# A six-block perceiver kernel: second ternary product from two float32r parts, norm weights applied while transposes are emptied, three scan states weighted outside VectorE

## The chip, the core and the metric

The kernel runs on one core of a Trainium2 chip. The metric is the device time of one launch in microseconds (us), the median of several runs. A core has five instruction queues that run side by side and wait for each other by semaphores: TensorE (PE, with its weight loads listed apart as PEld), VectorE (DVE), ScalarE (ACT), GpSimd (POOL) and SyncE (SP), which here issues all transfers. Each queue runs its instructions strictly in the order in which the program holds them.

## What is computed

128 sequences of 32 latent rows with 256 features (`x`) pass six residual blocks; each sequence also has a context of 257 rows with 256 features. Cut to what matters here:

```python
x = x + softmax_attention(ctx, layernorm(x))            # L0_xattn: latents attend to the context
x = x + mamba(layernorm(x))                             # L0_attn: per channel, 16 states
#   h = h * exp(A * d_t) + (x_t * d_t) * B ;  y_t = h @ C[0] ;  gate * (y + x*D) @ W_out + b
x = x + ternary_mlp(layernorm(x))                       # L0_ffn
#   h = gelu(x @ Wq_fc.T) ; h = layernorm(h)*ln_w + ln_b ; h @ Wq_proj.T   (Wq in {-1,0,1})
x = x + linear_attention(layernorm(x), ctx, ctx)        # L1_xattn
#   k = relu(ctx @ Wk + bk) + eps, scaled; k <- k^3 / |k^3| * |k| ; v = ctx @ Wv + bv
#   kv = k^T v ; z = 1 / (q . sum(k) + eps) ; out = (q kv) * z
x = x + latent_attention(layernorm(x))                  # L1_attn, 16 heads, decay on the scores
x = x + quantized_mlp(layernorm(x))                     # L1_ffn: 8-bit activations, ternary weights
```

All of it is float32 on the outside; the two linear maps of `quantized_mlp` run on whole numbers in bfloat16.

## The kernel before

The 4096 latent rows are 32 groups of 128 rows (four sequences to a group). Groups are taken in blocks of `BLOCKS = (2, 4, 4, 4, 4, 4, 4, 4, 2)`. A block goes through three stages: `context_group` for each of its groups (softmax attention over the context, then the keys and values of the later linear attention, `keys` and `keys_values`, which leave one small matrix `kvc` per group), `scan_block` for the block as a whole (four chunks `ic` of 128 channels, 16 states each), and `latent_group` for each group (`mlp`, `linear`, `attention`, `quantized_mlp`).

The order of instructions isn't the order of the text. Every call goes to a `Recorder`; `order` is a planner that places the recorded operations one by one. It has a price list for instructions (`ns_of`), due times for each part of the work (the table `DUE`), and factors (`PRICE`, `WINDOW` and others) with which it picks the next operation and, where an operation may run on several engines (`either`, `scaled`, `relu`, `copy`, `cast`, `minus_column`), its engine. Its result is a fixed order for each queue. Where the planner sees TensorE idle for longer than `GAP`, `keep_busy` puts in filler matmuls of constants (`onesb`, `identb`). All recorded instructions are issued from one line of the helper, so the profile shows L587 for them all, and they are told apart by the names of their tiles.

What the steps below touch:

- `cubed` (from L777): the scale `f` of a cubed key row from two sums of squares, `kn` (`ln` for queries): one GpSimd power of both sums (`kn<-kn,halves`), then their product (`kf<-kn`). `keys_values` (L1134) makes `u` (tile `ku`): ScalarE relu of the product `pkey`, GpSimd add of `e1`, two ScalarE squares with a row sum, GpSimd product, two squares again; then `vf`, the values scaled by `f`, and matmuls into `pk`.
- `context_group` (L1005) makes `kvc` from `pk` with two VectorE instructions.
- `norm` (L981): subtracts the row mean and multiplies by `rstd` on VectorE (`xn`). Used by `scan_block`, `attention` and `quantized_mlp`.
- `scan_block` (L1172): for each state `s`, ScalarE makes the decay `a`, VectorE runs the scan `h`. For `s < POOLED` GpSimd multiplies `h` by its weight and adds it to `some`; for the others VectorE does both in one instruction into `acc`. `POOLED` is 2, and `LATE_POOLED`, 6, in the last two blocks.
- `mlp` (L1240): the first ternary product (`ph<-w_fc,xT`) already takes its rows as two float32r parts. Then GELU (`hid`), eight transposes, two ScalarE copies out of PSUM (`hT`), eight float32 matmuls with `w_pr` (`pmlp`), into which `late_setup` has multiplied `ln_w` and from which it has taken the column mean.
- `linear` (L1276): `den`, `zf` and `y`, with the value bias `bv1` multiplied by the denominator on GpSimd.
- `quantize` and `quantized_mlp` (L1426, L1458): `xn` is multiplied by the factor `qm` and rounded; `q` is the bfloat16 result.

A float32 matmul shows as two records in the profile, a float32r or bfloat16 matmul as one. `R.together()` makes matmuls one unit for the planner.

Of the kernel before, what the change touches and what calls it, by code (L numbers as in the profile page):

```python
# [17 lines left out]
P = 128  # L18
# [24 lines left out]
def ns_of(engine, name, kw, out, ins, n):  # L43

    if engine == "vector":
# [4 lines left out]
        if name == "bn_aggr":  # L50
            return 118
        if name == "reciprocal":
            return 65 + 6.6 * n
        if name in ("tensor_scalar", "tensor_copy", "scalar_tensor_tensor"):
# [3 lines left out]
            start = (105 if in_psum(ins[0]) else 65) if both else 92  # L58
            return start + (0, 60, 175)[pointers] + (0.52 if fast else 1.04) * n
        return max(75 + 1.04 * n, 150)  # L60
    if engine == "scalar":
        pointers = is_ap(kw.get("scale")) + is_ap(kw.get("bias"))
        if n == BB * (LQ - 1):
            return 655
        rate, start = (0.834, 85) if in_psum(ins[0]) else (0.93, 65)
        return start + 75 * pointers + rate * n + (135 if kw.get("accum_out") is not None else 0)
    if engine == "gpsimd":
        if kw.get("op") == ALU.pow:
            return 400 + 150 * n
        if name in ("memset", "tensor_copy"):  # L70
            return 190 + 0.7 * n
        if name == "tensor_scalar":
            pointers = sum(is_ap(kw.get(k)) for k in ("scalar1", "scalar2"))
            return 195 + 75 * pointers + 0.83 * n
        if n == NH * LQ and shown(ins[1]).ap[-1][0] == 0:
            return 1030
        return 200 + (2.07 if n < 1000 else 1.7) * n
    if engine == "tensor":
# [7 lines left out]
        if not wide:  # L86
            return max(n / 2.4 + 3, 60)
# [180 lines left out]
class Recorder:  # L268
# [79 lines left out]
    def cost(self, engine, name, args, kw, all_reads, all_writes, all_bufs):  # L348
        if True:
            out = kw.get("out", args[0] if args else None)  # L350
            rest = list(args[1:] if "out" not in kw else args)
            rest += [v for k, v in kw.items() if k not in ("out", "accum_out")]
            ins = [a for a in rest if is_ap(a)]
            outs = [a for a in (out, kw.get("accum_out")) if is_ap(a)]
            full = dict(kw)
            if name == "tensor_scalar":
                full |= dict(zip(("scalar1", "scalar2"), args[2:4]))
            if name == "scalar_tensor_tensor":
                full |= dict(zip(("scalar",), args[2:3]))
            if name == "activation":  # L360
                full |= dict(zip(("func",), args[2:3]))
            if engine == "gpsimd" and name == "tensor_tensor":
                full |= dict(zip(("op",), args[3:4]))
            n = size_of(out)
            ns = ns_of(engine, name, full, out, ins, n)
            table = TABLES.get(full.get("func")) if name == "activation" else None
            tensors = [
                a for a in ins if (size_of(a) > 1 or name == "tensor_tensor") and not in_psum(a)
            ]
            locks = engine == "gpsimd" and len(ins) > 0  # L370
            if engine == "vector":
                two = name in ("tensor_tensor", "scalar_tensor_tensor", "tensor_tensor_scan")
                fast = name in ("tensor_scalar", "tensor_copy") and not in_psum(out)
                locks = len(tensors) > 1 if two else fast and len(tensors) > 0 and n > 64
# [228 lines left out]
PRICE = {"tensor": 0.0, "vector": 45.207809, "scalar": 8.002797, "gpsimd": 6.895979, "sync": 0.0}  # L603
WINDOW = 13.504066
SOONER = 0.067879
AHEAD = 0.971922
HORIZON = 1.829143
# [3 lines left out]
def perceiver_kernel(ctx: ExitStack, tc: tile.TileContext, t: dict, out: bass.AP):  # L611
# [30 lines left out]
    nc.gpsimd.memset(halves[:, 1, :], 0.5)  # L642
    ones = cst.tile([P, P], F32, name="ones")
# [58 lines left out]
    def t4k(shape, name):  # L702
        return ring("t4", 4).tile(shape, name)

    def t2k(shape, name, dtype=F32):
        return ring("t2", 15).tile(shape, name, dtype)
# [33 lines left out]
    bv1 = row("bv1", t["bv1"], D)  # L740
# [18 lines left out]
    w_pr = wts.tile([P, 8, D], F32, name="w_pr")  # L759
# [911 lines left out]
```

## Time and profile before

| | |
|---|---|
| time, median of 3 runs | 1727.35 us (1726.26 to 1727.77) |
| the profiled execution: its own time | 1720.31 us |
| its span, first to last instruction | 1718.6 us |
| DVE scans `h<-a,pproj` | 576 instructions, 615.9 us |
| ACT decays `a<-dl,a_neg` | 576, 368.9 us |
| PE `pval` and `pkey` records | 2 x 1024, 243.5 and 238.1 us |
| PE `pmlp` records | 512, 116.8 us |
| ACT table loads | 91, 116.8 us |
| DMA | 59.72 MB, mean 35 GB/s |

A group's busy time is the union of its instructions' spans; "mean" is one instruction's span from start to end. Instructions that follow each other on a queue overlap a little, so the time that one takes from its queue is a little less than its span. PE spans hold the latency to the result: a 256-column matmul of bfloat16 has a span of 0.27 us and starts 0.11 us after the one before it. So PE can show as busy while it waits. The 1.71 us between the span and the execution's own time lie outside the first and the last instruction.

### The profile page before, as it was taken

Reading aid. Unit: us, or ns where it says so; the run is one execution under the profiler, and the core shown is the slowest. Engines: PE = TensorE matmul, PEld = TensorE weight load, DVE = VectorE, ACT = ScalarE, POOL = GpSimd, SP = SyncE. Lnnn points to the kernel's source line nnn. Section 1 sums busy time; section 2 is a strip of 40 time slices with the busy share of each in tenths; the row PEclk is TensorE's granted clock in tenths of the full one; section 3 lists DMA queues with packets and bytes.
Section 4 is the critical chain, followed back from the end, with each engine's and each line's share of the span. In section 5 each row is a group of like instructions: output and inputs, shape, how many; then the busy total and the mean of one; then the engine's idle time right before and its main releaser. Section 6 shows DMA issues by size and latency. Waiting matters only on the chain.

```text
span 1718.6 us, 45554 instructions
## 1 busy us (share of the span) xinstructions
PE 1636.2 (95%) x17465; PEld 1209.2 (70%) x17495; DVE 1513.6 (88%) x2992; ACT 1406.5 (82%) x3441; POOL 1311.0 (76%) x2063
## 2 busy tenths in 40 slices
PE   9999999999999999999999999999999988888897
PEld 6777667767777777777777777766777656666664
DVE  5499599989997799969999998989999899999787
ACT  4588698979887898979988889888987888777676
POOL 6668667867688678887788777867887789688787
PEclk9999999999999999999999999999999999999999
DMA  8221100110110101000210011001100000000000
GB/s 252 79 76 60 30 28 30 35 58 1 35 57 2 35 14 57 8 30 13 70 29 30 4 45 55 10 30 35 42 35 30 2 11 16 4 5 2 5 9 22
DMA packets 44761, 59.72 MB, mean 35 GB/s; under 512 B 8704, under 2 KB 27008, under 8 KB 44544
## 3 DMA queue, kind: packets, MB, share of 16 engines
q1 hardware_dynamic: 44544, 56.81, 10.4%
q8 instruction: 138, 2.26, 0.6%
q14 instruction: 79, 0.65, 0.1%
HBM read 52.32 MB, written 4.19 MB: 33 GB/s over the span
## 4 chain that ended last, share of the span: by engine, by line
PE 41%; DVE 25%; ACT 16%; POOL 13%; issue 5%; DVEq 0%; POOLq 0%; ACTq 0%
DVE h L587 10%; PE pkey L587 7%; DVE acc L587 7%; PE pval L587 6%; PE pproj L587 5%; POOL ku L587 3%; ACT a L587 3%; PE pT L587 3%; PE pmlp L587 2%; ACT L587 2%; POOL some L587 2%; PE pk L587 2%; ACT ks L587 2%; PE pqa L587 2%; POOL rstd L587 1%
## 5 line engine op out<-in xcount | busy, mean ns | idle before, releaser
L587 DVE TENSOR_TENSOR_SCAN h<-a,pproj 128x512 f32<-128x512 f32 (+1 forms) x576 | 615.9, 1087 | 21.6 <-ACT a L587 11.2
L587 ACT ACTIVATE a<-dl,a_neg 128x496 f32<-128x496 f32 (+1 forms) x576 | 368.9, 665 | 82.7 <-DVE h L587 79.3
L587 DVE SCALAR_TENSOR_TENSOR acc<-h,w_st,acc 128x512 f32<-128x512 f32 (+1 forms) x436 | 299.2, 686 | 0.9
L587 PE MATMUL pval<-wkv,cT 128*128 128x256 f32 x1024 | 243.5, 383 | 2.8 <-DVE x L587 1.8
L587 PE MATMUL pkey<-wkv,cT 128*128 128x256 f32 x1024 | 238.1, 386 | 0.0
L587 ACT ACTIVATE ks<-ku 128x256 f32<-128x256 f32 x512 | 209.2, 414 | 13.6 <-POOL ku L587 10.2
L587 PEld LDWEIGHTS pkey<-wkv,cT 128*128 128x128 f32 x1024 | 189.3, 190 | 37.9 <-issue 14.8
L587 PEld LDWEIGHTS pval<-wkv,cT 128*128 128x128 f32 x1024 | 188.3, 190 | 35.3 <-issue 4.5
L587 POOL TENSOR_TENSOR ku<-ku,e 128x512 f32<-128x512 f32 x128 | 164.9, 1298 | 42.9 <-ACT ku L587 41.6
L587 POOL TENSOR_TENSOR ku<-ks,ku 128x512 f32<-128x512 f32 x128 | 163.2, 1283 | 20.5 <-ACT ks L587 18.9
L587 POOL TENSOR_TENSOR kn<-kn,halves 128x4 f32<-128x4 f32 x128 | 131.2, 1027 | 17.9 <-ACT ks L587 16.7
L587 ACT ACTIVATE vf<-pval,kf 128x256 f32<-128x256 f32 x256 | 107.8, 474 | 30.8 <-PE pval L587 17.5
L587 POOL TENSOR_TENSOR rstd<-rstd,halves 128x1 f32<-128x1 f32 x224 | 124.3, 558 | 7.0
L587 PE MATMUL pproj<-xTs,w_in 128*128 128x512 f32 (+1 forms) x288 | 123.7, 554 | 1.3 <-ACT vf L587 0.7
L587 ACT ACT_TABLE_LOAD x91 | 116.8, 1283 | 2.0 <-PE ph L587 0.5
L587 PE MATMUL pmlp<-w_pr,hT 128*128 128x256 f32 x512 | 116.8, 381 | 1.5 <-ACT hT L587 1.2
L587 POOL TENSOR_TENSOR some<-some,h 128x512 f32<-128x512 f32 (+1 forms) x104 | 115.1, 1107 | 3.1
L587 POOL TENSOR_SCALAR h<-h,w_st 128x512 f32<-128x512 f32 (+1 forms) x104 | 65.0, 628 | 60.4 <-DVE h L587 50.1
L587 POOL TENSOR_SCALAR rstd<-mv 128x1 f32<-128x1 f32 x224 | 45.5, 203 | 84.7 <-DVE mv L587 56.1
L587 PEld LDWEIGHTS pmlp<-w_pr,hT 128*128 128x128 f32 x512 | 95.8, 190 | 17.0 <-ACT hT L587 2.1
L587 ACT ACTIVATION_READ_ACCUMULATOR ks<-ku 128x1 f32 x512 | 100.1, 195 | 0.0
L587 ACT ACTIVATE ku<-pkey 128x512 f32<-128x512 f32 x128 | 73.0, 592 | 14.8 <-PE pkey L587 11.7
(289 smaller groups left out, 3836.1 us busy)
## 6 DMA issues: line engine op xcount, KB each, us to landing
cx<-in_ctx_dram SPq DMA_DIRECT2D x64, 512.0 KB
x<-in_x_dram SPq DMA_DIRECT2D x32, 128.0 KB
cr<-in_ctx_dram SPq DMA_DIRECT2D x128, 32.0 KB
out_dram<-x SPq DMA_DIRECT2D x32, 128.0 KB
vlz<-vl SPq DMA_DIRECT2D x128, 1.1 KB
w_in<-in_w_inT_dram SPq DMA_DIRECT2D x1, 1024.0 KB
raw_fc<-in_w_fcT_dram SPq DMA_DIRECT2D x2, 512.0 KB
raw_pr<-in_w_prT_dram SPq DMA_DIRECT2D x2, 512.0 KB
```

What stands on the lines that cost most here:

```text
L587: ins = getattr(engine, name)(*(traced(a) for a in args), **{k: traced(v) for k, v in kw.items()}).ins
```

## The change

- `mlp`: each half of the transposed `hid` leaves PSUM in four instructions of 128 columns, each multiplied by its part of `ln_w` (now rows on partitions); a copy to float32r (`hi`) and the difference (`lo`) follow; `pmlp` is 16 float32r matmuls with the ternary `w_pr`. The mean of the normalized rows is taken off behind the product, by one more VectorE instruction with `s1`. In `ph` the matmuls run part by part.
- `norm` is gone. The row mean is taken out of the weights (`centred` for `w_in`, `w_gate`, `wqa`, `wkd`) and rows are only scaled (`normed`), on VectorE, GpSimd or ScalarE as the planner picks. `scan_block` computes `rstd` for its groups in one pair of GpSimd instructions (`rs4`). `quantized_mlp` only subtracts the mean, and `rstd` goes into `amax` and `qm`.
- `POOLED` is 3, and the multiplication of a pooled state may run on ScalarE.
- `cubed`: VectorE reciprocal of one sum, a product, one power. In one of four sequences (`WHOLE`) VectorE does relu and add in one instruction. `kvc` gets the value bias at once (`bvc`, `vb`), and `linear` drops `den` and two of its steps. `bvc` comes by 16 transfers of 16 x 16 elements instead of one.
- The planner's price list, factors and due times are new, so the order changes everywhere. The ring `t4` has 3 buffers (4 before), `t2` has 17 (15 before).

The diff, cut to its core:

```diff
@@ cubed
-        powers = halves[:, 0:2, 0:n] if inverse else halves[:, 1:3, 0:n]
-        R.gpsimd.tensor_tensor(nrm, nrm, powers, ALU.pow)
         f = tiny(f"{tag}f", [P, n])
-        R.gpsimd.tensor_tensor(f, nrm[:, 0, :], nrm[:, 1, :], ALU.mult)
+        R.vector.reciprocal(f, nrm[:, 1 - inverse, :])
+        R.either.tensor_tensor(f, f, nrm[:, inverse, :], ALU.mult)
+        R.gpsimd.tensor_tensor(f, f, halves[:, 1, 0:n], ALU.pow)
@@ setup
+    centred(w_in, 2)
+    centred(w_gate, 2)
+    centred(wqa, 2)
@@ late_setup
-        R.vector.tensor_tensor(w_pr, w_pr, lnw.unsqueeze(2).to_broadcast([P, 8, D]), ALU.mult)
-        centred(w_pr, 8)
+        for col, dst, sign in ((lnb, s0, 1.0), (lnw, s1, -1.0)):
...
+            R.vector.tensor_scalar(dst, pS[:, 0:D], sign, None, ALU.mult)
@@ norm -> normed
-        xn = t1k([P, D], "xn")
-        R.vector.tensor_scalar(xn, xg, mv[:, 0:1], r, ALU.subtract, ALU.mult)
+    def normed(xg, r):
+        xn = t1k([P, D], "xn")
+        R.record({
+            "vector": ("tensor_scalar", (xn, xg, r, None, ALU.mult), {}),
+            "gpsimd": ("tensor_scalar", (xn, xg, r, 1.0, ALU.mult, ALU.mult), {}),
+            "scalar": ("activation", (xn, xg, AF.Copy), {"scale": r}),
+        })
@@ context_group
-        R.vector.tensor_scalar(kvc, v[:, 0], odd[:, 0:1], None, ALU.mult)
+        R.scaled(kvc, v[:, 0], odd[:, 0:1])
         R.vector.scalar_tensor_tensor(kvc, v[:, 1], odd[:, 1:2], kvc, ALU.mult, ALU.add)
+        vb = t1k([P, 2, GB, 16], "vb")
+        R.either.tensor_tensor(
+            vb, bvc.unsqueeze(2).to_broadcast([P, 2, GB, 16]),
+            kvc[:, :, :, 16:17].to_broadcast([P, 2, GB, 16]), ALU.mult,
+        )
+        R.either.tensor_tensor(kvc[:, :, :, 0:16], kvc[:, :, :, 0:16], vb, ALU.add)
@@ keys_values
+        if whole:
+            R.vector.scalar_tensor_tensor(u, z, 0.0, e12, ALU.max, ALU.add)
+        else:
+            R.relu(u, z)
+            R.gpsimd.tensor_tensor(u, u, e12, ALU.add)
@@ scan_block
                 if s < pooled:
-                    R.gpsimd.tensor_scalar(h, h, weight, 0.0, ALU.mult, ALU.add)
+                    R.record({
+                        "gpsimd": ("tensor_scalar", (h, h, weight, 0.0, ALU.mult, ALU.add), {}),
+                        "scalar": ("activation", (h, h, AF.Copy), {"scale": weight}),
+                    })
@@ mlp
-        hT = t4k([P, 8, P], "hT")
-        transposed(hid, hT, 8)
+        halved = []
+        for k in range(0, 8, 4):
...
+            for j in range(4):
+                R.scaled(hT[:, j, :], pt[:, j * P : (j + 1) * P], lnw[:, k + j : k + j + 1])
+            R.record({
+                "vector": ("tensor_copy", (hi, hT), {}),
+                "scalar": ("copy", (hi, hT), {}),
+                "gpsimd": ("tensor_copy", (hi, hT), {}),
+            })
+            R.either.tensor_tensor(lo, hT, hi, ALU.subtract)
+            halved += [(hi, k), (lo, k)]
         po = bank("pmlp")
         with R.together():
-            accumulate(po[:, 0:D], [(hT[:, c, :], w_pr[:, c, :]) for c in range(8)])
+            accumulate(
+                po[:, 0:D],
+                [(part[:, j, :], w_pr[:, k + j, :]) for part, k in halved for j in range(4)],
+            )
+        R.vector.scalar_tensor_tensor(po[:, 0:D], s1, mv[:, 0:1], po[:, 0:D], ALU.mult, ALU.add)
         R.vector.scalar_tensor_tensor(xg, po[:, 0:D], r2, xg, ALU.mult, ALU.add)
@@ linear
-        R.vector.tensor_copy(den, pv[:, :, 16])
...
-        R.gpsimd.tensor_tensor(
-            yv, bv1.rearrange("p (h k) -> p h k", k=16),
-            den.unsqueeze(2).to_broadcast([P, NH, 16]), ALU.mult,
-        )
-        R.vector.tensor_tensor(yv, pv[:, :, 0:16], yv, ALU.add)
-        R.vector.tensor_tensor(yv, yv, zf.unsqueeze(2).to_broadcast([P, NH, 16]), ALU.mult)
+        R.vector.tensor_tensor(
+            yv, pv[:, :, 0:16], zf.unsqueeze(2).to_broadcast([P, NH, 16]), ALU.mult
+        )
@@ quantize / quantized_mlp
-        R.vector.tensor_scalar(m, m, 127.0, None, ALU.mult)
+        R.either.tensor_scalar(m, m, 127.0, unit, ALU.mult, ALU.mult)
...
+        R.minus_column(xn, xg, mv[:, 0:1])
...
+        R.either.tensor_tensor(amax, amax, r, ALU.mult)
@@ constants
-POOLED = 2
+WHOLE = (0,)
+POOLED = 3
```

## The prediction

> **What bounds the kernel now.** First the page: busy shares, then the chain of work that ended last.
>
> ```profile
> PE 1636.2 (95%) x17465; PEld 1209.2 (70%) x17495; DVE 1513.6 (88%) x2992; ACT 1406.5 (82%) x3441; POOL 1311.0 (76%) x2063
> PE 41%; DVE 25%; ACT 16%; POOL 13%; issue 5%; DVEq 0%; POOLq 0%; ACTq 0%
> ```
>
> No engine sets the end alone: all four are on the chain. Next, busy time by stage, cut where the first scan starts (96 us) and where the last block's scans end (about 1600 us), and one stretch inside.
>
> ```profile
> 0.00:96.00 96.00, 91.57 (x816) 67.80 (x816) 46.44 (x124) 50.47 (x163) 60.44 (x110) 1.00 0.52 161
> 96.00:1600.00 1504.00, 1445.10 (x15241) 1071.28 (x15258) 1373.60 (x2604) 1278.28 (x3123) 1155.79 (x1785) 1.00 0.09 28
> 1600.00:1719.00 119.00, 99.53 (x1417) 70.14 (x1421) 93.55 (x265) 77.79 (x157) 94.73 (x169) 0.99 0.04 13
> 780.00:1180.00 400.00, 392.37 (x4269) 291.69 (x4277) 376.45 (x713) 354.43 (x846) 305.10 (x482) 1.00 0.10 31
> ```
>
> Columns: PE, PEld, DVE, ACT, POOL. In the middle PE shows 96.1% busy, DVE 91.3%, ACT 85.0%, POOL 76.8%; from 780 to 1180 us DVE holds 94.1% and ACT 88.6%. PE and DVE limit the middle together. ACT's longest wait is for DVE, by the view of waits (total, times, longest):
>
> ```profile
> ACT a L587 <- DVE h L587: 79.3, 102, 2.4
> ```
>
> In the tail no engine is full; dependences set the pace, and POOL is at 80%.
>
> **The change, part by part.** Counts are those of the changed program's queues; durations are means of the groups before. From these I take the overlap with the next instruction: 0.1 us on ACT (three decays of 0.50 us in a row take 1.29), 0.08 on DVE (two scans of 0.67 take 1.26).
>
> *PE.* The timeline gives the rates:
>
> ```profile
> 1628.68 3.62 PE L587 MATMUL pmlp<-w_pr,hT 128*128 128x256 f32 x16
> 1620.53 2.08 PE L587 MATMUL ph<-w_fc,xT 128*128 128x512 f32 x8
> 1703.75 1.03 PE L574 MATMUL poq<-onesb,identb 128*128 128x512 bf16 x4
> 1705.42 1.05 PE L587 MATMUL poq<-w,qT 128*128 128x256 bf16 x8 [0.64 <-ACT qT L587]
> ```
>
> Less the last one's span (0.38, 0.39, 0.39, 0.27), starts are 0.216 us apart for a float32 record of 256 columns, 0.241 for float32r of 512 (`ph`), 0.213 for bfloat16 of 512 and 0.111 of 256. The trace has no float32r matmul of 256 columns. Its bounds are 0.111 (bfloat16) and 0.216 (nothing gained per record); I take 0.111 plus the 0.028 that `ph` shows over bfloat16, 0.139. So 512 records of 0.216 become 512 of 0.139: -39 us (bounds -54 and 0). The setup adds six 512-column and two 256-column float32 matmuls (0.87 and 0.43), while eight for `lnw` replace eight for the mean of `w_pr`: +6. 31 fillers fewer (204 to 173) are -7 of busy time that stood in waits. PE's busy time: -40.
>
> [...]
>
> *DVE.* `acc`: 24 of 512 (0.66) and 4 of 256 fewer, -17. `xn` leaves: 96 x 0.415 and 32 x 0.49, -56. `y`, two steps and one back, -14. One `kvc`, `den` and part of `qm`: -14. Added: 161 reciprocals at 0.074, +12; 32 relu-and-adds from PSUM (as `pproj`, 0.67), +21; 32 times `s1` (as `x<-pmlp`, 0.39), +12; setup, five means and five subtractions for four weights, less what `w_pr` needed, +3. Sum -53.
>
> The `xn` means hold stalls: median and longest are in the second figure column.
>
> ```profile
> L587 DVE TENSOR_SCALAR xn<-x,mv,rstd x96: 360/406/1349, 44.4 to 1697.7; 128x256 f32<-128x256 f32 x96
> L587 DVE TENSOR_SCALAR xn<-xn,qm x32: 298/346/4076, 321.3 to 1699.3; 128x256 f32<-128x256 f32 x32
> ```
>
> Against the medians the stalls are 96 x 0.09 + 32 x 0.23 = 16 us of the 56; if they only move to other instructions the sum is -37. [...] The scans show none (longest 1.22 us at a mean of 1.21).
>
> *ACT.* `h` times its weight, 64 of 512 (as `a`, 0.61) and 30 of 256 (0.40): +51. `hT`, 256 of 128 columns: `vf` takes 0.474 at 256, and 128 columns are worth 0.108 by the two sizes of `a`, so 0.266 each: +68, less 64 copies of 0.495, +36 (without the overlap +62). `hi`, 38 of 512 (as `ea`, 0.53): +20. `xn`, 55 at 0.41: +23. `kvc`, 32 at 0.27: +9. 32 fewer relus: -16. Ten table loads fewer: -13. Sum +110, some 4 of it in the tail.
>
> *POOL.* `lo`, 64 x 1.28: +82. `some`, 24 x 1.275 + 4 x 0.73: +34. `hi`, 26 at about 0.6: +16. Smaller additions (mean subtraction, rounding, `vb`, `kvc`, `qm`, `amax`, `rs4`): +95. Removed: 66 weight products, -40; 32 adds of `e1`, -42; `kn` with four powers 1.03, with two 0.72, -39; queries -6; `rstd` -24; `y` -20. Sum +56. In the middle POOL would stand near 81%: hidden.
>
> *New waits.* The scale of a key row now visits DVE (`kf`), behind scans of 1.21 us, and GpSimd's power, ScalarE's `vf` and PE's `pk` queue up behind it. Keys run a stage ahead, and PE waited only 1.8 us for `kf` so far; I take 0. Uncovered, half a scan each is 128 x 0.6 = 77 us. `pmlp` waits for `lo`, and the context matmuls behind it on PE wait too; in the middle that is a matter of order, in the tail it counts below.
>
> *SP.* 15 transfers more at about 0.47 us each are 7 us of queue. Ahead of the first `plg` stand 58 issues, not 51, so it goes out at 39 us, not 36; its matmul started at 60 us. Cost 0; without that cover, 7.
>
> *Sum by stage.* Head: PE's first `w_in` projection has some 3 us less real work before it, but the next seven are spread among later context work: 0 (bounds -7 and +7). Middle, each engine at the density it keeps: PE (1445 - 40) / 0.961 = 1462; DVE (1374 - 53) / 0.913 = 1447; ACT (1278 + 106) / density. ACT becomes the fullest, and its density decides. Its longest wait is for a DVE that has less to do, and DVE shows that 94.1% can be held for 400 us; at that, 1471, or -33. At DVE's mean of 91.3% it is 1516, +12. I take 0.941. Tail: per group +0.5 (`hT`), +0.6 (`hi`), +1.3 (`lo`), +0.4 (`s1`), -1.2 (`pmlp`), -1.0 (`linear`); with POOL carrying 3.6 us more for each of some three groups, +4 (bounds -2 and +11). Together 0 - 33 + 4 = -29 against the profiled execution's 1720.3: 1691. The median of the runs is 7 us above that execution, so 1698.
>
> **The rivals.**
>
> *ACT hides its 110 us* (1690 or less). For it: 15% of the middle is idle on ACT. Against: it would need over 95%. PE then sets the middle, -42, with the tail 1689; with the 0.111 rate, 1674; with a head shorter by 7 too, 1667.
>
> *ACT becomes the bound: slower.* Place: scan stretches, where decays, squares, `vf` and now `h`, `hi` and `hT` share one queue. ACT has not held more than 88.6% in the 400 us shown. It decides from a density in the middle under 1384/1500 = 92.3%. At DVE's 91.3%: +12 + 4, 1743; at 88.6%, 1562, so +62, 1789. Against it: ACT's idle time was largely waiting for the engine that is relieved.
>
> *The float32r product gains nothing* (0.216 each). PE stays at 1445 - 1: 1503 for the middle, with the tail 1730, no change.
>
> **How the numbers follow.** Likeliest case 0.60, own range 1684 to 1722; ACT hides 0.10; ACT bounds 0.20; no gain on PE 0.10. Telling apart from no change takes about 0.2%, so 1723.9 to 1730.8 is "same". Faster: 0.57 + 0.10 + 0.03 = 0.70. Same: 0.02 + 0.02 + 0.04 = 0.08. Slower: 0.01 + 0.18 + 0.03 = 0.22. The range goes from 1662, just under the lowest of the second case, to 1743, the nearer price of the slower one; about 0.15 is left out.
>
> **What would show it.** Right: `pmlp` with 512 records about 0.14 us apart; DVE near 1460 us busy, ACT near 1515, POOL near 1365; ACT's waits for `h` well under 79 us; ACT at 93% or more between 300 and 1300 us. Wrong: `pmlp` starts 0.2 us apart; DVE waiting for `a` for tens of us (11.2 so far); ACT full and PE's waits longer; PE waiting at `pk` for `kf` or at `pmlp` for `lo`; a stretch after 1600 us much over 119 us.

## The result and the profile after

| | before | after |
|---|---|---|
| median of the runs (lowest to highest) | 1726.98 us (1721.69 to 1727.77, 9 runs) | 1731.58 us (1730.49 to 1733.57, 9 runs) |
| ratio to before, 95% interval | | 1.0035 (1.0027 to 1.0044) |
| profiled execution, its span | 1720.31, 1718.6 us | 1732.48, 1730.8 us |
| mean granted TensorE clock in it | 0.999 | 0.984 |

The change made the kernel 0.35% slower; 1698 us had been forecast. The profiled execution of before lies 7 us under its median and that of after 1 us over its own, so the two traces differ by 12 us where the medians differ by 5.

The page of the changed kernel, busy time by engine and then the chain of work that ended last:

```profile
PE 1614.0 (93%) x17484; PEld 1184.9 (68%) x17484; DVE 1467.7 (85%) x2933; ACT 1492.2 (86%) x3810; POOL 1356.1 (78%) x2214
ACT 32%; PE 27%; DVE 21%; POOL 15%; issue 5%; DMA 1%; DVEq 0%; POOLq 0%; ACTq 0%
```

Against before, DVE is down by 46 us (forecast 53), ACT up by 86 (110), POOL up by 45 (56), PE down by 22 (40). The loads moved as forecast, in sign and nearly in size; ACT's share of the chain doubled from 16 to 32%, and the time did not fall. PE and DVE are now busy for a smaller share of the span than before, ACT and POOL for a larger one.

The stretches, cut where the first scan starts, where the last scan starts, and at the end. The columns are PE, PEld, DVE, ACT and POOL busy, then clock, DMA share and GB/s. First the kernel before:

```profile
0.00:96.50 96.50, 92.07 (x848) 68.15 (x849) 46.93 (x124) 50.69 (x163) 60.44 (x110) 1.00 0.52 162
96.50:1609.30 1512.80, 1453.01 (x15393) 1076.66 (x15408) 1382.24 (x2628) 1286.12 (x3142) 1164.04 (x1796) 1.00 0.09 28
1609.30:1718.60 109.30, 91.11 (x1234) 64.42 (x1239) 84.42 (x242) 69.72 (x137) 86.47 (x158) 0.98 0.04 14
```

and the changed kernel, with two inner stretches:

```profile
0.00:83.80 83.80, 79.78 (x709) 59.93 (x710) 46.07 (x124) 42.52 (x142) 51.57 (x98) 1.00 0.49 151
83.80:1614.30 1530.50, 1444.01 (x15618) 1063.94 (x15620) 1348.77 (x2605) 1376.23 (x3517) 1208.94 (x1934) 0.99 0.09 30
1614.30:1730.80 116.50, 90.26 (x1169) 61.01 (x1158) 72.85 (x206) 73.41 (x152) 95.64 (x184) 0.92 0.04 12
300.00:1300.00 1000.00, 964.38 (x10742) 714.50 (x10735) 885.97 (x1679) 912.01 (x2322) 813.58 (x1325) 0.99 0.10 31
1300.00:1500.00 200.00, 170.64 (x1513) 116.08 (x1512) 174.52 (x298) 169.90 (x384) 152.17 (x234) 0.96 0.04 13
```

The head is 12.7 us shorter, the scan stretch 17.7 longer, the tail 7.2 longer: together the 12.2 us between the spans. In the scan stretch ACT was busy for 1376 us, close to the 1384 of the prediction, but in 1530.5 us: 89.9% dense, not 94.1. By the starts of the scans, the blocks keep the pace that they had: from the second block's first scan to the seventh's it is 942 us before and 945 after. What is lost on balance is lost behind 1340 us, and from there on no engine is near full: from 1300 to 1500 us they stand at 76 to 87%.

The view of waits of the changed kernel (total, times, longest):

```profile
POOL vb L588 <- DVE kvc L588: 39.1, 14, 5.3
DVE pproj L588 <- ACT some L588: 34.2, 14, 12.1
ACT a L588 <- DVE h L588: 33.2, 44, 4.8
PEld L575 <- issue: 33.1, 46, 6.2
POOL some L588 <- ACT h L588: 29.6, 19, 5.8
DVE h L588 <- ACT a L588: 24.9, 30, 2.3
```

and two rows of it in the kernel before:

```profile
DVE pproj L587 <- ACT some L587: 20.0, 11, 6.1
DVE h L587 <- ACT a L587: 11.2, 14, 2.1
```

ACT's waits for `h` fell from 79 to 33 us, as they should with a lighter DVE. In exchange DVE waits for ACT (`a` 24.9, 11.2 before; `some` 34.2, 20.0 before), and POOL waits for both in places that are new. L575 are the filler matmuls, put in to keep PE's clock up: it was 0.984 with them and 0.967 in the run without them below.

The second product itself, one instance on the timeline (start, us, engine, line, operation):

```profile
882.90 0.82 PE L588 MATMUL pmlp<-w_pr,hi 128*128 128x256 f32 x4
883.55 0.63 PE L588 MATMUL pmlp<-w_pr,lo 128*128 128x256 f32 x4
884.03 0.63 PE L588 MATMUL pmlp<-w_pr,hi 128*128 128x256 f32 x4
884.49 0.63 PE L588 MATMUL pmlp<-w_pr,lo 128*128 128x256 f32 x4
```

A run of four takes 0.63 us and one record spans 0.28, so starts are 0.117 us apart ((0.63 - 0.28) / 3): better than the 0.139 forecast, with a weight load for every one of them (512 loads, median span 0.188 us, for 512 matmuls). The first run here took longer, 0.82 us; over all of them in the trace the median distance of two starts is 0.117 us too. 512 records at 0.117 instead of 0.216 take 51 us out of PE's queue.

### The profile page after: what moved, and what is told of

Read it like the earlier page. It is cut to its first block, busy times and chain, and to the rows that moved or that the text cites. A ratio compares the mean times of both kernels' runs of the same rounds, so it can differ in the third digit from the quotient of the medians.

```text
span 1730.8 us, 46138 instructions
## 1 busy us (share of the span) xinstructions
PE 1614.0 (93%) x17484; PEld 1184.9 (68%) x17484; DVE 1467.7 (85%) x2933; ACT 1492.2 (86%) x3810; POOL 1356.1 (78%) x2214
## 4 chain that ended last, share of the span: by engine, by line
ACT 32%; PE 27%; DVE 21%; POOL 15%; issue 5%; DMA 1%; DVEq 0%; POOLq 0%; ACTq 0%
DVE h L588 9%; ACT a L588 6%; DVE acc L588 4%; PE pproj L588 4%; PE pkey L588 4%; PE pval L588 4%; ACT ks L588 4%; POOL ku L588 3%; ACT L588 3%; PE pT L588 2%; ACT hT L588 2%; ACT vf L588 2%; POOL some L588 2%; POOL rstd L588 2%; POOL lo L588 1%
## 5 line engine op out<-in xcount | busy, mean ns | idle before, releaser
L588 DVE TENSOR_TENSOR_SCAN h<-a,pproj 128x512 f32<-128x512 f32 (+1 forms) x576 | 615.6, 1088 | 38.6 <-ACT a L588 24.9
L588 ACT ACTIVATE a<-dl,a_neg 128x496 f32<-128x496 f32 (+1 forms) x576 | 370.0, 670 | 34.9 <-DVE h L588 33.2
L588 DVE SCALAR_TENSOR_TENSOR acc<-h,w_st,acc 128x512 f32<-128x512 f32 (+1 forms) x408 | 280.2, 687 | 0.8
L588 POOL TENSOR_TENSOR some<-some,h 128x512 f32<-128x512 f32 (+1 forms) x132 | 149.8, 1134 | 33.7 <-ACT h L588 29.6
L588 POOL TENSOR_TENSOR ku<-ku,e 128x512 f32<-128x512 f32 x96 | 123.4, 1293 | 40.0 <-ACT ku L588 37.5
L588 POOL TENSOR_TENSOR rstd<-rstd,halves 128x1 f32<-128x1 f32 x192 | 106.9, 558 | 3.8
L588 POOL TENSOR_TENSOR kf<-kf,halves 128x2 f32<-128x2 f32 x128 | 91.4, 716 | 3.9
L588 POOL TENSOR_TENSOR lo<-hT,hi 128x512 fp32r<-128x512 f32 x64 | 81.5, 1277 | 4.2 <-DVE acc L588 1.8
L588 DVE BATCH_NORM_STATS2 st<-x 128x6 f32<-128x256 f32 x192 | 78.7, 414 | 6.1 <-POOL x L588 2.9
L588 POOL TENSOR_SCALAR rstd<-mv 128x1 f32<-128x1 f32 x192 | 37.2, 194 | 59.4 <-DVE mv L588 33.6
L588 PE MATMUL ph<-w_fc,xT 128*128 128x512 f32 x256 | 75.8, 425 | 2.1 <-ACT xT L588 1.4
L588 ACT ACTIVATE hT<-pT,lnw 128x128 f32<-128x128 f32 x256 | 76.9, 398 | 0.4
```

The lines of the kernel that those rows point to most:

```text
L588: ins = getattr(engine, name)(*(traced(a) for a in args), **{k: traced(v) for k, v in kw.items()}).ins
```

## The experiments

Ratios are to the kernel before, with 95% intervals, each against runs of before on the same chip; the changed kernel's own 1.0035 is what the variants of it are held against. It was not measured again beside them, so a variant of it whose interval reaches into 1.0027 to 1.0044 is not told apart from it. One per cent is 17 us. "In its own order" means that the planner's order and its choice of engines stay as they were, and only what is named differs: a replanned order would differ in every queue at once.

### Is it the fillers and the clock?

Theory A at this point: ACT's load and its waits made the loss. Rival B: the fillers, sized by planned gaps, are late and stand in the way. Rival C: the fillers hold the clock, and the changed plan has its idle time elsewhere. The changed kernel held about 57 us at half clock in stretches of 3.4 us and its multiples, the one before 4.5.

Fillers left out of the changed kernel, and out of the kernel before:

```diff
-GAP, FILL = 600.0, 0.7
+GAP, FILL = 600.0, 0.0
```

> The changed kernel with the same order of instructions, without its 173 filler matmuls. Theory A (ScalarE has become the fullest engine and sets the pace): the fillers stand in PE's waits, so within 3 us of the changed kernel's 1731.6. Theory B (the loss of the last 400 us is made by fillers that run late, at half clock, on the path: 5.6 us before a ph at 1477 us, 3.1 at 1372, some 1.5 each at 1381, 1566 and 1568): 8 to 12 us shorter. Theory C (the fillers hold the clock, which fell from 0.999 to 0.984): the clock falls further, below 0.97, and the kernel is 5 us or more longer.

Measured: 1734.17 us, ratio 1.0061 (1.0039 to 1.0083), clock 0.967.

> The kernel before with the same order, without its 204 fillers. Theory C (fillers hold the clock): its clock falls from 0.999 to about 0.98 and it gets 5 to 15 us longer than 1727. Theory A: the clock may fall, but the time stays within 3 us. Theory B: shorter by the 5 us of fillers that the chain of before names at its start (pwqk, 5.4 us) or less.

Measured: 1738.52 us, 1.0084 (1.0069 to 1.0099), clock 0.974. So the fillers are worth 0.84% (15 us) in the kernel before, all of it behind 1500 us: the first scan of the last block starts at 1501.8 us against 1501.2, its last one 9.6 us later. In the changed kernel they are worth 0.26% by the medians, which the intervals don't tell from nothing. The traces show two opposite things in it: without fillers the first scan of the last block starts 9.0 us earlier (1490.8 against 1499.8), and the rest takes 10.7 us longer (241.7 against 231.0, to the end of the span). Why they delay is in the chain of the changed kernel (start, us, what):

```profile
1476.58 0.74 ACT vf L588 x2
1477.32 0.04 issue
1477.36 5.59 PE ph L575 x17
1482.95 0.94 PE ph L588 x4
```

and on its timeline, where the bracket is the idle time before an instruction and what ended it:

```profile
1477.36 5.59 PE L575 MATMUL ph<-onesb,identb 128*128 128x512 bf16 x17 [6.00 <-ACT vf L588]
```

The 17 fillers write the bank that the matmul behind them is to write. PE stood idle for 6 us until `vf` had emptied that bank, at half clock by then (0.50 from 1474.2 to 1480.9 us), and only then ran the fillers, 0.33 us each: they came after the wait that they were to fill, in front of `ph`.

Three tries to use this. First, up to 307 fillers in 72 places where the changed kernel's own trace showed gaps (where a place had planned ones too, the larger number); second, the planned ones without those ahead of the last block's first chunk (60 of the 173 stay in the trace, so 113 are left out, not the 89 of the expectation); third, a choice by whether the gap had grown with them:

```diff
-            if op.engine == "tensor" and op.gap > GAP:
-                self.keep_busy(op)
+            if op.engine == "tensor":
+                self.unit += 1
+                self.keep_busy(op)
...
+        n = max(n, IDLE.get(self.unit, 0))
```

> The changed kernel in its own order, with filler matmuls put where its own trace showed TensorE idle for over 0.9 us in a row (72 places, 307 fillers of 0.22 us in all, beside the planned ones); nothing else differs. It holds 57 us at half clock, before 4. Theory C (part of the loss is clock: the changed plan's idle stretches are not where its fillers are): the granted clock returns to 0.995 or more, and at the price that the kernel before showed without fillers (15 us for 0.025 of clock) the time falls by 8 to 10 us, to a ratio of 0.997 to 0.999. Theory A (the loss is other engines' load and waits, the clock falls only because TensorE idles): the clock returns, and the time stays within 3 us of the changed kernel's, ratio 1.002 to 1.005.

Measured: 1740.49 us, 1.0096 (1.0081 to 1.0111), clock 0.993. Neither theory: the clock came back and the time rose by 0.6%. Some nine places had gaps that grew by over 0.6 us against the changed kernel, the one at `ph` above by another 5.3.

```diff
-            if op.engine == "tensor" and op.gap > GAP:
+            unit += op.engine == "tensor"
+            if op.engine == "tensor" and op.gap > GAP and unit > 1427:
                 self.keep_busy(op)
```

> The changed kernel in its own order, with the planned filler matmuls ahead of the first one of the last block's chunks (about 1490 us) left out, 89 of 214, and those behind kept. The run without any fillers was 9.0 us ahead of the changed kernel at the first scan of the last block (1490.8 against 1499.8 us) and lost 10.7 from there on (238.6 us instead of 227.9). Theory B (fillers are sized by planned gaps, and in the stretch from 1340 to 1490 the input comes before they are through, so that they delay; behind 1490 they hold the clock): both gains add up, 7 to 10 us under the changed kernel, ratio 0.997 to 1.000. Theory C (fillers only hold the clock, and the 9 us were another difference): the clock falls in the middle and the time stays within 3 us of the changed kernel's, ratio 1.002 to 1.006.

Measured: 1725.14 us, 1.0013 (1.0002 to 1.0024), clock 0.977: 0.22% under the changed kernel, between the two expectations.

```diff
-        n = max(n, IDLE.get(self.unit, 0))
+        n = IDLE.get(self.unit, 0)
```

> The changed kernel in its own order, each filler place chosen anew by the traces with and without fillers: kept or added where the gap on TensorE stayed the same length with them (44 places, most behind 1590 us), left out where it grew (1354, 1359, 1422 and the like in the list of matmul groups: 2.8, 2.3 and 7.0 us longer with the planned fillers). If the fillers' own delay was the larger part of what the changed kernel lost (the gaps at filler places are 27.5 us shorter without fillers, and the clock costs part of that back), the time comes to 1717 to 1723 us, ratio 0.996 to 0.999, with a clock of 0.975 to 0.985. If others' work closes in on the gaps, it stays at the run with late fillers alone, 1.000 to 1.003.

Measured: 1730.34 us, 1.0032 (1.0022 to 1.0042), clock 0.984. A miss. Its profiled execution was its fastest, 1723.9 us; the others took some 7 us more, which one trace can't show. Fillers and clock have a real effect (0.84% in the kernel before, 0.22% here with late fillers alone), but no setting tried turned the changed kernel into a faster one than before. None of them held the clock without putting more work into PE's queue, so what the 57 us at half clock cost by themselves is not shown.

### What is an engine's relief worth in the changed kernel?

Each of these takes work off one engine, in the changed kernel's own order.

```diff
+                    R.ops[-1].left_out = ("scalar",)
                     R.gpsimd.tensor_tensor(some, some, h, ALU.add)
...
+            if op.engine in getattr(op, "left_out", ()):
+                continue
```

> The changed kernel with its order kept; ScalarE's 94 multiplications of pooled scan states by their weights are left out (the states are added unweighted). That is 64 x 0.61 + 30 x 0.40 = 51 us less of ScalarE's queue. Theory A: ScalarE sets the pace from 300 to 1600 us, so 30 to 50 us shorter than 1731.6. Rival (all engines share the path in proportion, ScalarE with 32% of the chain): 10 to 18 us shorter. If ScalarE is hidden: within 4 us.

Measured: 1721.81 us, 0.9986 (0.9976 to 0.9996): 51 us less on ACT are worth 8.5 us. Its largest wait, 33.2 us in the changed kernel, shows where most of the relief went:

```profile
ACT a L590 <- DVE h L590: 63.4, 88, 4.7
```

```diff
             R.either.tensor_tensor(lo, hT, hi, ALU.subtract)
+            R.ops[-1].left_out = ("vector", "gpsimd")
+            lo.buf.instead = hi.buf
```

> The changed kernel with its order kept; the 64 differences lo are left out and the matmuls of the low part read hi a second time, so PE's work is the same. GpSimd loses 64 x 1.28 = 82 us of its queue and pmlp no longer waits for them. Theory A: GpSimd is hidden, within 5 us of 1731.6. Theory D (the longer way from hid to pmlp costs the tail, GpSimd 83% busy after 1600 us): 6 to 15 us shorter, most of it behind 1300 us. Proportional sharing (GpSimd 15% of the chain): about 10 shorter, spread evenly.

Measured: 1727.56 us, 1.0020 (1.0010 to 1.0031): 82 us less on POOL are worth 2.6 us, which the intervals don't tell from nothing.

```diff
                         acc, h, weight, some if s == pooled else acc, ALU.mult, ALU.add
                     )
+                    if s in (8, 12):
+                        R.ops[-1].left_out = ("vector",)
```

> The changed kernel in its own order, with 2 of the 13 weighted sums over states of each chunk on VectorE left out (states 8 and 12; 10 in the last block), 72 instructions of 0.69 us: 49 us off VectorE's queue, the like of the 51 us that were taken off ScalarE's for 8.5 us of time. If VectorE bounds the middle (theory: its 53 us less were worth most of their size), 30 to 45 us less, ratio 0.977 to 0.986. If it is one of four engines that take turns (its share of the chain is 21 to 25%), 10 to 14 us less, ratio 0.995 to 0.998.

Measured: 1726.16 us, 1.0015 (1.0005 to 1.0025): 49 us less on DVE are worth 3.4 us, less than its share of the chain.

And the float32r rate undone, in the same order:

```diff
+        calls = R.ops[-1].ways["tensor"][0]
+        calls[:] = [
+            (name, (dst, a.bitcast(F32), b.bitcast(F32)), {"start": i == 0, "stop": i == 7})
+            for i, (name, (dst, a, b), _) in enumerate(calls[0:4] + calls[8:12])
+        ]
```

> The changed kernel in its own order, the second product done again in float32 from one part: the copy hi keeps float32, the subtraction lo is left out, and in the place of sixteen float32r matmuls stand eight float32 ones, two passes each. The result is that of the reference. Beside the run without lo (ratio 1.0020) it differs in TensorE's work alone: 51 us more in its queue, by the spacings of 0.117 and 0.216 us. If TensorE's relief was worth what the prediction counted (about 0.8 us of time per us of queue in the middle), it is 25 to 40 us slower than the run without lo, ratio 1.017 to 1.025. If it was worth its share of the chain of waits (27 to 41%), 14 to 20 us, ratio 1.010 to 1.014. If TensorE waits for others anyway, under 5 us, ratio up to 1.005.

Measured: 1754.10 us, 1.0175 (1.0154 to 1.0197), 26.7 us above the run without `lo`: 0.52 us of time for each of 51 us put back into PE's queue. Its chain, beside the 27% of PE in the changed kernel:

```profile
PE 46%; ACT 22%; DVE 18%; POOL 9%; issue 4%; DMA 0%; DVEq 0%; ACTq 0%; POOLq 0%
```

So the changed order rests on the faster product; and none of the three loads taken away is worth a fifth of its size. The last one moves load:

```diff
+                    R.ops[-1].moved = "gpsimd"
...
+            op.engine = getattr(op, "moved", op.engine)
             engine = getattr(self.nc, op.engine)
```

> The changed kernel in its own order, the 94 multiplications of the states by their weights that the planner gave to ScalarE moved to GpSimd, in the same place of the order: 51 us off ScalarE, some 60 us more on GpSimd (0.65 us each); the result is the reference's. Without them ScalarE's relief was worth 8.5 us, and 82 us less on GpSimd was worth 2.6. If GpSimd has the room (78% busy, its work hidden), 4 to 9 us less than the changed kernel, ratio 0.998 to 1.001. [...]

Measured: 1771.60 us, 1.0276 (1.0259 to 1.0292). POOL, which could lose 82 us for almost nothing, can't take 54 more (1356.1 to 1410.4 busy): 2.4% over the changed kernel. The run moved the load and its place on POOL's queue at once and doesn't say which of them cost the time.

### What is the order worth?

Both kernels planned anew with one planner setting exchanged:

```diff
-WINDOW = 13.884593
+WINDOW = 13.504066
```

> The changed kernel with one setting of its planner, the window in which an instruction of earlier due time is preferred, at the value of the kernel before (13.504 instead of 13.885 us); the arithmetic is the same, the order is planned anew. It shows what another order of the same work is worth. If the time hangs on the engines' loads, it stays within 0.2% of the changed kernel, ratio 1.001 to 1.006. If the loss is an accident of this order in the last 400 us, it lands anywhere from 0.995 to 1.02.

Measured: 1839.87 us, 1.0669 (1.0633 to 1.0706).

```diff
-WINDOW = 13.504066
+WINDOW = 13.884593
```

> The kernel before with the planner's window at the value of the changed kernel (13.885 instead of 13.504 us): the same work, planned anew. In the changed kernel the reverse step was worth 6.3%. If any replanning away from the settings that a plan was made with costs tens of us (the order is the result of a search and fits one set of settings), 1.02 to 1.10. If only the changed kernel's work is that sensitive, within 1% of the kernel before.

Measured: 1838.58 us, 1.0675 (1.0650 to 1.0700). The changed kernel so planned has nearly the same instructions and this page line, and this stretch:

```profile
PE 1680.8 (91%) x17677; PEld 1209.1 (66%) x17677; DVE 1476.7 (80%) x2934; ACT 1507.7 (82%) x3807; POOL 1358.1 (74%) x2226
300.00:1300.00 1000.00, 932.10 (x9981) 675.31 (x9980) 827.78 (x1564) 861.22 (x2153) 754.10 (x1232) 0.98 0.10 30
```

The same work and the same engines, a setting 2.7% off, and ACT's density between 300 and 1300 us is 86.1 instead of 91.2%. So density is not set by the load alone; the order sets it too. For the same reason no part of the change was put alone into a replanned kernel: such a run would show the plan.

### Loads in the order of the kernel before

Here the prediction's terms are put, one at a time and with nothing else, into the order that it reasoned from. Half of the second product left out:

```diff
             accumulate(po[:, 0:D], [(hT[:, c, :], w_pr[:, c, :]) for c in range(8)])
+        calls = R.ops[-1].ways["tensor"][0]
+        calls[:] = calls[0:3] + calls[7:8]
```

> The kernel before in its own order, with 4 of the 8 float32 matmuls of the second product left out: 55 us off TensorE's queue (32 times 4, two passes of 0.216 us each), the like of what the change takes off it, and nothing added anywhere. If TensorE's relief is worth what the prediction counted in the middle (33 us of 46 with the other engines free to close up), 30 to 45 us less, ratio 0.974 to 0.983. If the fixed order of the other engines holds the pace, and TensorE's work is worth more when added (0.52 us per us in the changed kernel) than when taken away, 5 to 20 us less, ratio 0.988 to 0.997.

Measured: 1731.84 us, 1.0041 (1.0025 to 1.0058): slower, with 55 us less to do. Its page, and its cores:

```profile
PE 1609.0 (93%) x17209; PEld 1174.3 (68%) x17239; DVE 1516.8 (88%) x2992; ACT 1406.5 (81%) x3441; POOL 1311.5 (76%) x2063
core 0: 1729.8 us, clock 0.986
```

PE's busy time fell by 27 us, not 55. Half-clock stretches of 3.4 us now stand all along the span (14 of them, 48 us, and 1.6 at the end; 4.5 before): some 45 us more at half clock are up to 22 us of PE's work given back. DVE, ACT and POOL are busy for the same time, and none moved up into the room. So this run is PE's relief together with a lower clock; the relief at full clock was not measured.

Two weighted sums of each chunk left out on DVE, as in the run above, and then both together:

> The kernel before in its own order, with 2 weighted sums over states of each chunk on VectorE left out (states 8 and 12), 72 instructions of 0.69 us: 49 us off VectorE, the like of the 46 that the change takes off it, and nothing added. If VectorE's relief is worth what the prediction counted (with TensorE's, 33 us in the middle), 15 to 35 us less, ratio 0.980 to 0.991. If the fixed order holds the pace, as in the changed kernel (3.4 us for 49), 0 to 6 us less, ratio 0.996 to 1.001.

Measured: 1714.20 us, 0.9940 (0.9924 to 0.9956): 10 us for 49, between the two expectations. Clock 0.998.

> The kernel before in its own order with both left out: 4 of the 8 float32 matmuls of the second product (55 us of TensorE) and 2 weighted sums of each chunk (49 us of VectorE), nothing added. The prediction's sum gave 33 us in the middle for such a relief of both. If each engine covers for the other, and only both together free the path, 25 to 45 us less, ratio 0.974 to 0.986. If the order of the lists, not the load of these two, holds the pace, between the run with half the second product (1.0041) and 6 us under the kernel before, ratio 0.996 to 1.004.

Measured: 1716.73 us, 0.9951 (0.9936 to 0.9966): 8 us for 55 on PE and 49 on DVE, just past the second range. PE's relief, with the clock at 0.990, adds nothing to DVE's.

Now load added. A copy in place on ACT between scan and weight of each pooled state:

```diff
+            if getattr(op, "copied", None) is not None:
+                h = traced(op.copied)
+                extra = self.nc.scalar.activation(h, h, AF.Copy).ins
```

> The kernel before in its own order, with a copy of the state in place on ScalarE put between VectorE's scan and GpSimd's scaling of each pooled state: 88 instructions, some 55 us more on ScalarE (0.73 us for 512 columns, less in the two half blocks), and one hand-over more for each pooled state; the result is the reference's. If ScalarE hides it (it was 82% busy, and 87% between 300 and 1300 us), 0 to 10 us more, ratio 1.000 to 1.006. If ScalarE's list is in step with the others, so that added work costs its share or more, 15 to 50 us more, ratio 1.009 to 1.03.

Measured: 1774.97 us, 1.0294 (1.0277 to 1.0310). The copies were 104 (72 of 512 columns, 32 of 256), 58 us: 51 us of time. Its largest wait:

```profile
POOL h L598 <- ACT h L586: 120.9, 75, 12.4
```

In the kernel before, POOL waited 50.1 us for these states, straight from DVE. The longer wait is the hand-over that each copy put in, so load and hand-over had to be told apart: the decay of each pooled state computed twice on ACT, and the weight on POOL followed by a product with 1.0.

```diff
-            for name, args, kw in op.ways[op.engine][0]:
+            for name, args, kw in op.ways[op.engine][0] + getattr(op, "more", []):
...
+                if s < pooled:
+                    R.ops[-1].more = R.ops[-1].ways["scalar"][0]
```

> The kernel before in its own order, the exponential of each pooled state (104 of 576) done twice on ScalarE with the same operands: 67 us more on ScalarE (72 of 0.71 us, 32 of 0.50), no engine more in the chain; the result is the reference's. If ScalarE's load itself costs (it is in step with the others, its slack is in waits that the order gives away), 45 to 65 us more, ratio 1.026 to 1.038. If the copies cost through their hand-over and ScalarE has room (18% idle), 0 to 15 us more, ratio 1.000 to 1.009.

Measured: 1760.74 us, 1.0202 (1.0180 to 1.0225): 35 us for 67, less than expected for a pure load price and far more than for a hidden one. Its page and chain:

```profile
PE 1649.8 (94%) x17465; PEld 1215.0 (69%) x17495; DVE 1516.9 (86%) x2992; ACT 1468.0 (83%) x3545; POOL 1314.7 (75%) x2063
PE 39%; ACT 25%; DVE 23%; POOL 8%; issue 5%; SPq 0%; DMA 0%; DVEq 0%; ACTq 0%; POOLq 0%
```

```diff
+                    R.ops[-1].more = [("tensor_scalar", (h, h, 1.0, 0.0, ALU.mult, ALU.add), {})]
```

> The kernel before in its own order, each pooled state on GpSimd multiplied by 1.0 once more after its weight: 104 instructions, 64 us more on GpSimd (72 of 0.69 us, 32 of 0.45), no engine more in the chain; the result is the reference's. The change adds 45 us there. If GpSimd hides it (76% busy; in the changed kernel 82 us less were worth 2.6), 0 to 10 us more, ratio 1.000 to 1.006. If its list is in step as well, 25 to 60 us more, ratio 1.015 to 1.035.

Measured: 1771.60 us, 1.0269 (1.0253 to 1.0285): 46 us for 64, on the engine with the most idle time. Its page and chain:

```profile
PE 1658.9 (94%) x17465; PEld 1219.4 (69%) x17495; DVE 1524.6 (86%) x2992; ACT 1409.1 (80%) x3441; POOL 1371.4 (77%) x2167
PE 34%; DVE 25%; POOL 22%; ACT 14%; issue 4%; DVEq 0%; POOLq 0%; ACTq 0%
```

POOL is 77% busy at the end, and its share of the chain went from 13 to 22%. The share of busy time did not tell what an addition costs. In one table, us of time per us of queue:

| load | in the order of | us of queue | us of time | per us |
|---|---|---|---|---|
| PE taken off | before | -55 | +7 | none |
| DVE taken off | before | -49 | -10 | 0.2 |
| PE and DVE taken off | before | -55, -49 | -8 | |
| ACT added | before | +67 | +35 | 0.52 |
| ACT added with a hand-over | before | +58 | +51 | 0.87 |
| POOL added | before | +64 | +46 | 0.72 |
| ACT taken off | after | -51 | -8.5 | 0.17 |
| DVE taken off | after | -49 | -3.4 | 0.07 |
| POOL taken off | after | -82 | -2.6 | 0.03 |
| PE added | after | +51 | +27 | 0.52 |

The us of queue are counts times mean durations. The busy times on the pages moved by less: 27 us for the first row, 35 for the second, 62, 44 and 60 for the three additions in the order of before, 43, 39, 81 and 43 for the last four. By these the additions cost 0.57 to 1.16 and the reliefs 0 to 0.29.

Two things limit these prices. Each addition to ACT and POOL stands at one place, on the way of the pooled states from decay to `some`, so a longer way of these states is a rival to the load itself; no run put the same load elsewhere. In the doubled decays DVE's waits for `a` grew from 11.2 to 24.9 us, in the doubled products its waits for `some` from 8.9 to 23.2. And the clock fell in all three, to 0.993, 0.987 and 0.985, which is part of their time.

On the page of before PE is 95% busy by its matmuls and 70% by its weight loads, DVE 88%. Of the reliefs in this order DVE's was the one that brought time, but only 10 us for 49; PE's brought none.

## Why the prediction was wrong

**The rate on PE was right, and its bounds held.** 0.117 us lies between 0.111 and 0.216; the rival in which the product gains nothing, at 0.216, fell, on the timeline and by the 27 us that undoing it costs. PE's busy time fell by 22 us and not 40: half-clock stretches grew from 4.5 to about 57 us, which is worth up to some 26 us of PE's work, a term that the sum did not have.

**DVE, ACT, POOL.** -46, +86, +45 against -53, +110, +56. DVE lies between the prediction's -53 and its -37 for stalls that move. On ACT and POOL the new groups are there as counted (column order as before: busy and mean ns):

```profile
L588 ACT ACTIVATE hT<-pT,lnw 128x128 f32<-128x128 f32 x256 | 76.9, 398 | 0.4
L588 ACT ACTIVATE h<-h,w_st 128x512 f32<-128x512 f32 x64 | 46.6, 730 | 10.4 <-DVE h L588 10.2
L588 ACT CAST hi<-hT 128x512 fp32r<-128x512 f32 x38 | 24.9, 663 | 0.3
L588 POOL TENSOR_TENSOR lo<-hT,hi 128x512 fp32r<-128x512 f32 x64 | 81.5, 1277 | 4.2 <-DVE acc L588 1.8
```

With each instruction of ACT counted until the next one starts, the terms of the +110 measure +112 together (`hT` 67 for 68, its old copies -32 for -32, weights 53 for 51, `xn` 24 for 23, `hi` 21 for 20, `kvc` 10 for 9, relus -17 for -16, table loads -13 for -13). The page shows +86 because the older instructions follow each other more closely (the decays take 333 us so counted, 345 before). One slip in the working: "+62" without the overlap takes the overlap off one side only; off both it is +56, and nothing rests on it.

**The step that failed is the middle: "each engine at the density it keeps", with ACT at 0.941.** It gave -33 us; the scan stretch came out 17.7 us longer, with ACT at 89.9%: its load was right (1376 us for 1384), the time that holds it was not. The 94.1% was DVE's, held over 400 us of another order; a density was carried from one engine to another and from one order to the next. The runs show two things in its place. First, the reliefs that it counted on, put alone into the order of before, gave 8 us together and PE's gave none, part of it to a lower clock; so neither PE nor DVE limited the middle in the sense of the sum. That the four lists are in step, each waiting for the others in turn, is the reading that fits these runs. Second, added work of the kind that it let ACT and POOL hide is dear in that order, at the place where it was tried: 0.52 to 0.87 us per us on ACT, 0.72 on POOL, which the prediction had as "hidden" at near 81%. At these prices, and if they simply add up and hold at other places (no run shows that they do), the change in the order of before would come to -8 + 86 x 0.52 + 45 x 0.72 = +69 us. It came to +5. That the new order, made for the new loads, won back the rest is argued, not shown: the change was not run in the old order. That an order can be worth so much is shown by the two runs with an exchanged setting, 6.3 to 6.8% longer each way.

**The rivals.** "ACT becomes the bound: slower" named the right side and the right condition (89.9% is under its 92.3%), but not the mechanism: 51 us off ACT gave 8.5 us, so ACT is no bound in the changed kernel. "ACT hides its 110 us" needed over 95% and 1690 us or less; it fell with the 89.9% and the time. "The float32r product gains nothing" landed nearest in time, 1730, for a reason that is not so.

**Head and tail.** The head was put at 0 with bounds of 7 either way and gained 12.7, outside them: the first scan starts at 83.8 us, where the new order placed it; no run took that apart, and the lead, 10.5 us still at the eighth block's first scan, is gone at that block's last. The tail was put at +4 (-2 to +11) and is +7.2, with the clock there at 0.92.

**Waits.** The wait for `kf` was taken as 0: POOL waits 24.0 us in all for DVE's `kf` and DVE 18.7 for `ks`, far under the 77 of the uncovered case; whether part of it lies on the path was not tried. ACT's waits for `h` fell as foretold, and "DVE waiting for `a` for tens of us", named as a sign of error, is what came.

**What stays open.** How the 5 us divide between the fillers in the wrong places (0.2% by the run with late fillers alone, nothing by the fitted ones), the 57 us at half clock and the order at large is not settled. None of the runs that compute the whole result was faster than the kernel before.

## What to carry to other kernels

In a kernel whose engines' lists were ordered by a search, take no gain from an engine's busy share: price an edit by leaving the order as it is, taking the work out or adding it twice, and timing that; here reliefs were worth 0 to 0.2 of their length and additions 0.5 to 0.9 at the places tried, on the emptiest engine too. By such prices an edit that adds more on two engines than it takes off two others starts with a loss that a new order has to win back. Judge a new order against a second one of the same work before reading a few tenths of a per cent as the worth of an edit.

## What the hardware showed

- Work taken off PE cost time in the order of before: with 55 us less, half-clock stretches of 3.4 us appeared all along the span, clock 0.986 instead of 0.999, and the kernel took 0.41% longer.
- Such a stretch also came with PE 79% busy ahead of it. In that run, the 3.4 us ahead of one and the stretch itself (columns as in the stretches above):

```profile
614.08:617.49 3.41, 2.68 (x26) 1.59 (x25) 3.41 (x11) 3.39 (x6) 1.27 (x3) 1.00 0.03 6
617.49:620.90 3.41, 3.41 (x9) 2.68 (x9) 3.41 (x6) 3.38 (x7) 3.41 (x4) 0.50 0.02 3
```

Among the matmuls there are some of few rows (`pk<-vlz,plg` of 4 and `pkey<-bk,onesb` of 3 stand at this place of the order), and PE has two idle gaps of 0.51 and 0.22 us; ahead of the 14 stretches of 3.4 us it shows 12 to 79%.
- Float32r matmuls of 256 columns, each with its own weight load, started 0.117 us apart in a burst; float32 records of that size, two to a matmul, stood at 0.216.
- The clock alone is not the time: with more fillers it rose to 0.993 from 0.984 and the kernel took 0.6% longer. In the kernel before, all fillers together were worth 15 us, the last 220 us of the span holding nearly all of it:

```profile
1500.00:1735.00 235.00, 195.93 (x2293) 143.28 (x2291) 189.08 (x504) 156.34 (x337) 178.59 (x313) 0.87 0.02 7
```

This is the kernel before without fillers: PE is granted 0.87 of its clock there, against 0.99 from 1500 us on with them.
